# Score tables stored node by node and read in one transfer, edge types checked on ScalarE, a different order at the ends of the second stage

## The chip, the cores and the metric

The kernel runs on one core of a Trainium2 chip. The time is device microseconds from launch to end, the median of the runs shown. One more execution was taken by the hardware profiler; all durations below are from it.

## The reference

Four graph layers on a batch of 128 graphs of 128 nodes with 128 features each; every layer is `x = x + layer(relu(layernorm(x)), adj)`. The first layer is the one that the change is about:

```python
D = abs(x[:, :, None, :] - x[:, None, :, :])        # every pair of nodes
h = einsum('bijc,oc->bijo', D, W1) + b1             # 64 channels
m, v = mean(h, (0, 1, 2)), var(h, (0, 1, 2))        # over the whole batch
h = leaky((h - m) / sqrt(v + EPS) * g1 + be1)       # slope 0.01
s = einsum('bijo,uo->biju', h, W2)[..., 0] + b2
s = where(adj > 0, s, NEG)
y = (softmax(s) @ x) @ Wg.T + bg
y = leaky((y - mean(y, (0, 1))) / sqrt(var(y, (0, 1)) + EPS) * gg + beg)
out = concat([x, y], 2) @ Wt.T + bt
```

Layers 1 and 2 are attention over the same edges with eight heads and with one. Layer 3 picks one of eight score matrices by the value of `adj`, where -1 means no edge. The inputs of this case hold only 0 and 1, so that two of the eight types are enough. The kernel decides that at run time from a number called `types`.

## The kernel before

**Stage A** (0 to about 1255 us) works through pairs of nodes. Scores are symmetric, so each graph needs only half its pairs: node i with the 63 or 64 nodes that follow it, cyclically. A graph's 128 nodes are cut in NQ = 4 quarters of QR = 32; `block(b, q)` makes the absolute differences of one quarter in a tile `d` (VectorE at L541 or GpSimd at L544, then ScalarE at L547), multiplies by W1 in `ph` (TensorE, L558) and copies to `v` (ScalarE, L568); VectorE takes the statistics (L573). A graph's `v` (128 x 4064 floats, 2032 KB) goes to DRAM (L522). The last KEEP = 8 graphs stay in SBUF, in the 8 buffers of the pool `pairs`.

**Stage B** (about 1263 to 2107 us) turns pairs into attention, 8 graphs (GS) to a *score table*, 16 tables, the first one for the graphs that are still in SBUF. For each graph (`graph_scores`): load `v` (SyncE's queue, L654); normalise two parts of 1528 columns on ScalarE (L659), leaky on VectorE (`leaky_part`, L418); a relu of the last quarter on ScalarE (L663); 20 matmul records of TensorE (L684) that add the graph's rows to the table's PSUM bank `sc`. For each table (`score_table`): VectorE adds a bias to make `us` (L703); four DMAs of GpSimd's queue, one for each quarter, write `us` to a DRAM tile `s` in a skewed pattern (L713); four more read it back as rows of nodes, `u` (L726), each to 32 partitions. DRAM is the place where columns of pairs become rows of nodes. Then `attention` for each half table of 4 graphs: GpSimd folds the columns (L767), TensorE sums with the transpose and the mask in `pl` (L774 to L777), softmax on VectorE and ScalarE (L782 to L792), two more matmuls, and `yt` is stored (L808) with its statistics (L812). The generator `edges` brings `adj` (L738) and h (L753) of 4 graphs, makes the mask `negm` on VectorE (L742), and on GpSimd adds a*a - a of each edge number to `sum_odd` in four operations (L746 to L750). After the last table VectorE and TensorE reduce `sum_odd` to `types` (L836 to L841).

**Stage C** (about 2107 us to the end) starts with a branch on `types` (L1306). `layers` then runs the rest in 32 groups of 4 graphs. `load(g)` issues four DMAs (L981 to L987) into pool `c_in` with 3 buffers of each; group g's generator asks for group g+1.

The order of instructions of TensorE, ScalarE, VectorE and GpSimd is fixed ahead by `in_order`. It is a planner: generators yield an engine, a planned duration, and the buffers taken and freed, and the planner always emits the step that can begin first by its own clock. `yield "wait", t` only moves that clock. Each engine then executes its list strictly in that order, so a step planned too early blocks all that stands behind it. In `score_table` the planned waits are 3.0 after the writes and 14.0 after the reads. SyncE is not planned; its DMAs go out in program order. GpSimd's own DMAs stand in GpSimd's list.

Of the kernel before, what the change touches and what calls it, by code (L numbers as in the profile page):

```python
# [9 lines left out]
F32 = mybir.dt.float32  # L10
I32 = mybir.dt.int32
# [148 lines left out]
def kernel(ctx: ExitStack, tc: tile.TileContext, x, adj, w, out):  # L160
# [46 lines left out]
    nc.sync.dma_start(w_slide[0:64, 30:31], w2_col)  # L207
    nc.sync.dma_start(w_slide[64:128, 31:32], w2_col)
# [157 lines left out]
    QS = GS * QR * (W + 1)  # L366
    scores_d = [dram.tile([NQ, QS], F32, tag=f"s{i}", name=f"s{i}") for i in range(2)]

# [47 lines left out]

    def leaky(engine, out, v, slope):
        engine.scalar_tensor_tensor(out, v, slope, v, ALU.mult, ALU.max)  # L418
# [4 lines left out]
    with tc.tile_pool(name="h_pool", bufs=1) as h_pool, tc.tile_pool(name="pairs", bufs=B_V) as b_v:  # L423
# [10 lines left out]
        with tc.tile_pool(name="a2", bufs=2) as a2, tc.tile_pool(  # L434
# [13 lines left out]
            zero = a_d.tile([P, QR * 64], F32, tag="d", name="zero")[:, 0 : NQ * QS // P]  # L448
            nc.gpsimd.memset(zero, 0.0)
            for sd in scores_d:  # L450
                flat_sd = bass.AP(
                    tensor=sd.tensor, offset=sd.offset, ap=[[NQ * QS // P, P], [1, NQ * QS // P]]
                )
                nc.sync.dma_start(flat_sd, zero)
# [71 lines left out]
            def block(b, q, made):  # L526
# [22 lines left out]
                ph = a_ph.tile([P, 2, 512], F32, tag="ph", name="ph")  # L549
                for part in range(1 if q else 4):  # L550
                    for t in range(2):
                        for a in range(2):
                            k = (2 * t + a) * n
                            if part == 0:
                                wt, x_ = w1T if q else w1T2, d[:, k : k + n]
                            else:
                                wt, x_ = us[:, part - 1, :], both[:, k : k + n]
                            nc.tensor.matmul(  # L558
                                ph[64 * a : 64 * a + 64, t, 0:n], wt, x_,
                                start=part == 0, stop=q > 0 or part == 3,  # L560
                            )
# [20 lines left out]
            with tc.manual_schedule(engines=ORDERED):  # L582
# [19 lines left out]
                po, own[0:64, :], w_slide[0:64, 30:31].to_broadcast([64, GS * QR]),  # L602
# [3 lines left out]
            for sd in scores_d:  # L606
                for q in range(NQ):
                    diagonal = bass.AP(
                        tensor=sd.tensor, offset=sd.offset + q * QS + QR * q,
                        ap=[[QS, 1], [W + 1, GS * QR]],  # L610
                    )
                    nc.sync.dma_start(diagonal, own_row)


        with tc.tile_pool(name="b2", bufs=2) as b2p, tc.tile_pool(name="b_s", bufs=2, space=PSUM) as b_s, tc.tile_pool(
            name="b_ps", bufs=6, space=PSUM
        ) as b_ps:
            scores, tables, masks = {}, {}, {}
            sum_odd = b2p.tile([P, GB, P], F32, tag="sum_odd", name="sum_odd", bufs=1)
            nc.gpsimd.memset(sum_odd, 0.0)  # L620
# [10 lines left out]
                shift_ps, h_bi[0:64, :].to_broadcast([64, P]), w_slide[0:64, 30:31],  # L631
# [9 lines left out]
            def leaky_part(part, n):  # L641
                yield DVE, 0.15 + 0.00112 * n, "", ""
                leaky(nc.vector, part, part, 0.01)

            def graph_scores(order, i):
# [3 lines left out]
                if b in here:  # L649
                    v = here.pop(b)  # L650
                else:
                    yield DMA, 5.9, "v", ""
                    v = b_v.tile([P, NPAIR], F32, tag="v", name="v")
                    nc.sync.dma_start(v, pairs_d[b])  # L654
                lin = first[NQ - 1]
                for a, e in ((0, lin // 2), (lin // 2, lin)):
                    yield ACT, 0.2 + 0.00092 * (e - a), "", ""
                    part = v[:, a:e]
                    nc.scalar.activation(part, part, AF.Identity, bias=h_bi, scale=h_sc)  # L659
                    yield "fork", leaky_part(part, e - a)  # L660
                yield ACT, 1.1, "r", ""
                r = b2p.tile([P, 1024], F32, tag="r", name="r", bufs=B_R)
                nc.scalar.activation(  # L663
                    r[:, 0 : NPAIR - lin], v[:, lin:NPAIR], AF.Relu, bias=h_bi, scale=h_sc
                )
                yield "join",
                if i:
                    yield "after", ("w2", order[i - 1])
# [4 lines left out]
                for t in range(2):  # L673
                    k = 2 * (b % GS) + t
                    begins, ends = i == t == 0, i == GS - 1 and t == 1
                    for q in [*range(NQ), NQ]:
                        rows = slice(QR * min(q, NQ - 1), QR * min(q, NQ - 1) + QR)
                        n = 8 * width[min(q, NQ - 1)]
                        if q < NQ:
                            z = v[:, first[q] + t * n : first[q] + t * n + n]  # L680
                        else:
                            z = r[:, t * n : t * n + n]
                        wz = w_slide if q < NQ - 1 else w_line if q < NQ else w_relu
                        nc.tensor.matmul(  # L684
                            sc[rows, 0:n], wz[:, 30 - 2 * k : 62 - 2 * k], z,
                            start=begins and q < NQ, stop=ends and q != NQ - 1,
                            tile_position=(0, rows.start),
                        )
# [4 lines left out]
            def score_table(k):  # L693
# [14 lines left out]
                for q in range(NQ):  # L708
                    skewed = bass.AP(
                        tensor=sd.tensor, offset=sd.offset + q * QS + QR * q + 1,  # L710
                        ap=[[8 * (W + 1), QR], [W + 1, 8], [1, width[q]]],
# [8 lines left out]
                yield POOL, 2.6, "", "us"  # L720
                for q in range(NQ):
                    by_row = bass.AP(
                        tensor=sd.tensor, offset=sd.offset + q * QS,
                        ap=[[W, QR], [QR * (W + 1), GS], [1, W]],
                    )
                    nc.gpsimd.dma_start(u[QR * q : QR * q + QR], by_row)  # L726
                tables[k] = u
                yield "wait", 14.0
# [4 lines left out]
            def edges(g):  # L733
# [9 lines left out]
                yield POOL, 3.8, "", "adj"  # L743

                adf = b2p.tile([P, GB, P], F32, tag="adf", name="adf", bufs=1)
                nc.gpsimd.tensor_copy(adf, adjs)  # L746
                odd = b2p.tile([P, GB, P], F32, tag="odd", name="odd", bufs=1)
                nc.gpsimd.tensor_tensor(odd, adf, adf, ALU.mult)
                nc.gpsimd.tensor_tensor(odd, odd, adf, ALU.subtract)
                nc.gpsimd.tensor_tensor(sum_odd, sum_odd, odd, ALU.add)  # L750
# [11 lines left out]
                yield "done", ("edges", g)  # L762

            def attention(g, u):
# [43 lines left out]
                nc.gpsimd.dma_start(y_d[g], yt)  # L808
                yield DVE, 1.5, "", "yt"
# [3 lines left out]
                nc.vector.bn_aggr(y_mv[:, g, :], y6.rearrange("p a b -> p (a b)"))  # L813

            makers = []

            for k in [NB // GS - 1, *range(NB // GS - 1)]:
                makers += [partial(edges, k * GS // GB + g) for g in range(GS // GB)]
                order = sorted(range(GS * k, GS * k + GS), key=lambda b: b not in here)
                makers += [partial(graph_scores, order, i) for i in range(GS)]  # L820
                makers.append(partial(score_table, k))
            two = dict.fromkeys(("sc", "us", "adj", "negm", "zg", "e", "eT", "yt", "ht"), 2)
            with tc.manual_schedule(engines=ORDERED):
# [3 lines left out]

            n_parts = NB // GB
            mean, var = mean_var(
                b2p, [(1.0 / n_parts, y_mv[:, :, 0], y_mv[:, :, 1])], n_parts  # L830
            )
            affine(b2p, y_sc, y_bi, mean, var, None, gg, beg)


            odd_p = b2p.tile([P, 1], F32, tag="odd_p", name="odd_p")
            nc.vector.tensor_reduce(odd_p, sum_odd.rearrange("p g j -> p (g j)"), AX.X, ALU.max)  # L836
            pt = b_ps.tile([1, P], F32, tag="pb", name="odd_ps")
            nc.tensor.transpose(pt, odd_p, ident)
            odd_1 = b2p.tile([1, 1], F32, tag="odd_1", name="odd_1")
            nc.vector.tensor_reduce(odd_1, pt, AX.X, ALU.max)  # L840
            nc.vector.tensor_scalar(types, odd_1, 1.0, None, ALU.min)  # L841
# [5 lines left out]
    def layers(simple):  # L847

        with tc.tile_pool(name="c_in", bufs=3) as c_in, tc.tile_pool(
# [126 lines left out]
            loaded = {}  # L976

            def load(g):
                b0 = g * GC
                xg = c_in.tile([P, GC, P], F32, tag="xg", name="xg")  # L980
                nc.sync.dma_start(xg, x_t[:, b0 : b0 + GC, :])  # L981
                ad = c_in.tile([P, GC, P], I32, tag="adj", name="adj")
                nc.sync.dma_start(ad, adj_t[:, b0 : b0 + GC, :])
                yt = c_in.tile([P, GC, P], F32, tag="yt", name="yt")
                nc.sync.dma_start(yt, y_d[g])
                ht = c_in.tile([P, GC, P], F32, tag="ht", name="ht")
                nc.sync.dma_start(ht, h_d[g])  # L987
                loaded[g] = xg, ad, yt, ht
# [95 lines left out]
            def group(g):  # L1084
                b0 = g * GC
                xg, ad, yt, ht = loaded.pop(g)
                if g + 1 < NB // GC:
                    load(g + 1)
# [210 lines left out]
            load(0)  # L1299
# [49 lines left out]
```

## Time and profile before

| | us |
|---|---|
| median of 3 runs | 3228.68 (3226.74 to 3233.18) |
| the profiled execution | 3225.39 |
| its span, first to last instruction | 3223.1 |

| window | length | TensorE busy | VectorE busy | ScalarE busy | GpSimd busy |
|---|---|---|---|---|---|
| 0 to 1200 | 1200 | 1093.20 | 1157.88 | 1154.19 | 1092.99 |
| 1290 to 1690 | 400 | 327.62 | 299.94 | 309.51 | 130.06 |
| 1690 to 2050 | 360 | 296.39 | 264.10 | 271.38 | 131.30 |
| 2170 to 3130 | 960 | 906.66 | 771.52 | 759.12 | 209.57 |

A busy time that is close to its window's length marks the engine that sets the pace there. Where none is close, as in the second and third rows, waits set it.

### The profile page before, as it was taken

The numbers are of one execution on the slowest core, as the hardware profiler recorded it, in microseconds if no ns is written. First come the engines' busy times: TensorE is split into PE (matmuls) and PEld (weight loads), VectorE is DVE, ScalarE is ACT, GpSimd is POOL, SyncE is SP. The second block draws the span as 40 slices with busy tenths as digits, with TensorE's granted clock in tenths as the row PEclk, the third lists the DMA queues.
The fourth block names the chain that finished last, engine by engine and source line by source line (L and its number), as shares of the span: only waits on it lengthen the run. The fifth ranks groups of instructions, "written<-read, shape, count | busy, mean of one in ns | idle before, by whom it ended". The sixth has DMA issues, their size and how long they took to land.

```text
span 3223.1 us, 46662 instructions
## 1 busy us (share of the span) xinstructions
PE 2841.3 (88%) x17077; PEld 1552.3 (48%) x17129; DVE 2683.3 (83%) x4729; ACT 2656.7 (82%) x3018; POOL 1666.3 (52%) x1130
## 2 busy tenths in 40 slices
PE   6999999999999997878788887779999999999996
PEld 2333333333333332323333333357777787877875
DVE  6999999999999998868677786567787888887864
ACT  5999999999999998968687777547777777877774
POOL 5999999999999996233324233221222122312211
PEclk8999999999999998989999999879999999999997
DMA  3565555555555541999999999340111111111000
GB/s 126 232 248 227 230 237 233 233 222 246 245 227 231 235 188 60 394 374 388 374 375 396 365 394 371 129 124 11 43 47 38 43 37 43 44 40 40 11 11 12
DMA packets 151743, 606.48 MB, mean 188 GB/s; under 512 B 16401, under 2 KB 99794, under 8 KB 120786
## 3 DMA queue, kind: packets, MB, share of 16 engines
q1 hardware_dynamic: 140242, 569.86, 45.8%
q0 software_dynamic: 11264, 33.53, 3.2%
q8 instruction: 140, 2.29, 0.3%
q14 instruction: 97, 0.79, 0.1%
HBM read 322.74 MB, written 280.61 MB: 187 GB/s over the span
## 4 chain that ended last, share of the span: by engine, by line
PE 21%; DVE 17%; DMA 13%; ACT 4%; issue 4%; POOL 2%; SPq 0%; POOLq 0%; DVEq 0%; ACTq 0%
DMA u<-s 7%; PE pa L1052 6%; DMA s<-us 4%; DVE v L418 3%; PE po L964 2%; DVE p L920 1%; PE ps L1071 1%; PE pp L1064 1%; PE z L916 1%; PE pl L774 1%; PE ph L1194 1%; DVE s L886 1%; DVE e L792 1%; POOL s L713 1%; DVE xh L973 1%
## 5 line engine op out<-in xcount | busy, mean ns | idle before, releaser
L544 POOL TENSOR_TENSOR d<-he 128x2016 f32<-128x2016 f32 (+1 forms) x288 | 1021.8, 3576 | 74.7 <-ACT v L568 62.4
L558 PE MATMUL ph<-d,w1T 128*64 128x512 f32 (+1 forms) x4096 | 934.9, 595 | 85.2 <-ACT d L547 41.0
L547 ACT ACTIVATE d<-d 128x2016 f32<-128x2016 f32 (+1 forms) x384 | 740.6, 1931 | 0.1
L573 DVE BATCH_NORM_STATS2 six<-v 128x6 f32<-128x504 f32 (+1 forms) x1024 | 631.7, 671 | 8.2 <-ACT v L568 5.0
L558 PEld LDWEIGHTS ph<-d,w1T 128*64 128x64 f32 x4096 | 296.5, 137 | 621.0 <-issue 366.4
L568 ACT COPY v<-ph 128x1024 f32<-128x1024 f32 (+1 forms) x512 | 517.4, 1035 | 10.6 <-PE ph L558 10.4
L893 POOL TENSOR_TENSOR rs<-ve,nhalf 128x4 f32<-128x4 f32 x96 | 120.0, 1250 | 777.2 <-DVE ve L890 595.8
L541 DVE TENSOR_TENSOR d<-he,pt 128x2048 f32<-128x2048 f32 (+1 forms) x224 | 506.2, 2260 | 9.7 <-PE ph L558 9.7
L418 DVE SCALAR_TENSOR_TENSOR v<-v 128x1528 f32<-128x1528 f32 x256 | 439.8, 1763 | 28.6 <-ACT v L659 28.1
L659 ACT ACTIVATE v<-v,h_bi,h_sc 128x1528 f32<-128x1528 f32 x256 | 410.7, 1652 | 7.0 <-DVE h_bi L415 7.0
L684 PE MATMUL sc<-v,w_slide 128*32 128x512 f32 (+1 forms) x1536 | 334.7, 604 | 42.5 <-DVE v L418 42.5
L1052 PE MATMUL pa<-vals,p 128*128 128x99 f32 (+2 forms) x2048 | 259.2, 283 | 15.6 <-DVE p L920 11.6
L1052 PEld LDWEIGHTS pa<-vals,p 128*128 128x128 f32 x2048 | 253.5, 200 | 33.8 <-DVE p L920 15.4
L684 PE MATMUL sc<-v,w_line 128*32 128x504 f32 x512 | 262.1, 594 | 0.0
L684 PE MATMUL sc<-r,w_relu 128*32 128x504 f32 x512 | 259.1, 588 | 0.0
L920 DVE SCALAR_TENSOR_TENSOR p<-p,q 128x1024 f32<-128x1024 f32 (+1 forms) x192 | 205.6, 1078 | 49.6 <-ACT q L1039 24.8
L558 PE MATMUL ph<-both,us 128*64 128x512 bf16 x1536 | 189.3, 379 | 0.0
L1038 ACT ACTIVATE p<-z 128x1024 f32<-128x1024 f32 x128 | 133.3, 1041 | 38.2 <-PE z L916 37.8
L782 DVE TENSOR_REDUCE mx<-pl 128x4 f32<-128x512 f32 x32 | 21.9, 685 | 170.4 <-PE pl L777 170.4
L786 ACT ACTIVATE e<-e 128x512 f32<-128x512 f32 x32 | 20.2, 631 | 172.8 <-DVE e L784 172.8
L558 PEld LDWEIGHTS <-us 128*64 128x64 bf16 x1536 | 100.6, 110 | 116.8 <-issue 73.2
L663 ACT ACTIVATE r<-v,h_bi,h_sc 128x1008 f32<-128x1008 f32 x128 | 156.2, 1221 | 0.8 <-PE sc L684 0.8
(255 smaller groups left out, 4693.4 us busy)
## 6 DMA issues: line engine op xcount, KB each, us to landing
v<-v SPq DMA_DIRECT2D x240, 2032.0 KB, 9.1
xg<-in_x SPq DMA_DIRECT2D x64, 256.0 KB, 3.1
ht<-h SPq DMA_DIRECT2D x64, 256.0 KB, 6.1
u<-s POOLq DMA_DIRECT2D x64, 192.0 KB, 13.2
h<-he SPq DMA_DIRECT2D x32, 256.0 KB, 3.1
adj<-in_adj POOLq DMA_DIRECT2D x32, 256.0 KB, 8.8
y<-yt POOLq DMA_DIRECT2D x32, 256.0 KB, 8.0
adj<-in_adj SPq DMA_DIRECT2D x32, 256.0 KB, 2.9
```

Source lines behind the costliest of these rows:

```text
L418: engine.scalar_tensor_tensor(out, v, slope, v, ALU.mult, ALU.max)
L541: nc.vector.tensor_tensor(dv, later, own, ALU.subtract if q else ALU.max)
L544: nc.gpsimd.tensor_tensor(dv, later, own, ALU.subtract)
L547: nc.scalar.activation(d[:, 0 : 4 * n], d[:, 0 : 4 * n], AF.Abs)
L558: nc.tensor.matmul(ph[64 * a : 64 * a + 64, t, 0:n], wt, x_, start=part == 0, stop=q > 0 or part == 3,)
L568: nc.scalar.copy(v.rearrange("p (t e) -> p t e", t=2), ph[:, :, 0:n])
L573: nc.vector.bn_stats(made["six"][:, 2 * q + t, :], v[:, t * n : t * n + n])
L659: nc.scalar.activation(part, part, AF.Identity, bias=h_bi, scale=h_sc)
L663: nc.scalar.activation(r[:, 0 : NPAIR - lin], v[:, lin:NPAIR], AF.Relu, bias=h_bi, scale=h_sc)
L684: nc.tensor.matmul(sc[rows, 0:n], wz[:, 30 - 2 * k : 62 - 2 * k], z, start=begins and q < NQ, stop=ends and q != NQ - 1, tile_position=(0, ...
L920: nc.vector.scalar_tensor_tensor(p, p, FLOOR, q, ALU.max, ALU.max)
L1052: nc.tensor.matmul(pa_all[:, h * (DH + 1) : h * (DH + 1) + n], p[:, h, :], vals_all[:, e : e + n], start=True, stop=True,)
```

## The change

- The DRAM tile of a table is now 128 rows of 8 x 193 floats, a row for each node, and the 8 graphs lie one after the other in it. The read is one DMA with 128 partitions in place of four with 32; both read 1024 pieces of 768 bytes. The writes stay four DMAs of the same 256-byte pieces, but a partition's 8 pieces now lie in rows that are 4 nodes apart, and neighbouring partitions are 772 bytes apart.
- For that, stage A's matmuls take rows r, r+4, r+8, ... of a quarter (a strided view of `d` and `both`) instead of 8 rows in sequence, and W2 is put in other columns of `w_slide`.
- The planned costs change: after the read 8.0 instead of 14.0, its issue 1.2 instead of 2.6, the `v` load 5.2 instead of 5.9, a leaky part 0.00105 instead of 0.00112 for each column. The relu and the normalising steps become forks of their own.
- `edges` forks `of_types`: one ScalarE operation, the sum over a row of (a - 0.5) squared, in place of the four on GpSimd. A row with only 0 and 1 gives 128, anything else more.
- `y_norm`, `edge_types` and `first_inputs` become chains in the planner. The last one loads group 0's four inputs of stage C to a pool `late` while stage B still runs; `load(1)` then takes the place of `load(0)`.
- In the first table two graphs are put ahead of the `edges` steps.

```diff
-    QS = GS * QR * (W + 1)
-    scores_d = [dram.tile([NQ, QS], F32, tag=f"s{i}", name=f"s{i}") for i in range(2)]
+    ROW = GS * (W + 1)
+    scores_d = [dram.tile([P, ROW], F32, tag=f"s{i}", name=f"s{i}") for i in range(2)]
...
+                every4 = "p (r x j) -> p x r j"
+                by_part = d[:, 0 : 4 * n].rearrange(every4, x=4, j=w_)
+                both_by_part = both.rearrange(every4, x=4, j=64)
...
-                            k = (2 * t + a) * n
+                            k = 2 * t + a
                             if part == 0:
-                                wt, x_ = w1T if q else w1T2, d[:, k : k + n]
+                                wt, x_ = w1T if q else w1T2, by_part[:, k]
                             else:
-                                wt, x_ = us[:, part - 1, :], both[:, k : k + n]
+                                wt, x_ = us[:, part - 1, :], both_by_part[:, k]
...
                     skewed = bass.AP(
-                        tensor=sd.tensor, offset=sd.offset + q * QS + QR * q + 1,
-                        ap=[[8 * (W + 1), QR], [W + 1, 8], [1, width[q]]],
+                        tensor=sd.tensor, offset=sd.offset + QR * q * ROW + 1,
+                        ap=[[W + 1, QR], [4 * ROW, 8], [1, width[q]]],
                     )
...
                 yield "wait", 3.0
-                yield POOL, 2.6, "", "us"
-                for q in range(NQ):
-                    by_row = bass.AP(
-                        tensor=sd.tensor, offset=sd.offset + q * QS,
-                        ap=[[W, QR], [QR * (W + 1), GS], [1, W]],
-                    )
-                    nc.gpsimd.dma_start(u[QR * q : QR * q + QR], by_row)
-                tables[k] = u
-                yield "wait", 14.0
+                yield POOL, 1.2, "", "us"
+                by_row = bass.AP(
+                    tensor=sd.tensor, offset=sd.offset, ap=[[ROW - 1, P], [W + 1, GS], [1, W]]
+                )
+                nc.gpsimd.dma_start(u, by_row)
+                yield "wait", 8.0
...
-                yield POOL, 3.8, "", "adj"
...
-                nc.gpsimd.tensor_copy(adf, adjs)
-                odd = b2p.tile([P, GB, P], F32, tag="odd", name="odd", bufs=1)
-                nc.gpsimd.tensor_tensor(odd, adf, adf, ALU.mult)
-                nc.gpsimd.tensor_tensor(odd, odd, adf, ALU.subtract)
-                nc.gpsimd.tensor_tensor(sum_odd, sum_odd, odd, ALU.add)
+                yield "fork", of_types(g, adjs)
...
+            def of_types(g, adjs):
+                yield ACT, 0.65, "", "adj"
+                nc.scalar.activation(
+                    adjs.bitcast(F32), adjs, AF.Square, bias=nhalf[:, 0:1], accum_out=squares[:, g : g + 1]
+                )
+                to_see.remove(g)
+                if not to_see:
+                    yield "done", "types"
...
+            def first_inputs():
+
+                yield "after", ("loaded", order[-1])
+                for dst, src in zip(early, inputs(0)):
+                    if src is y_d[0]:
+                        yield "after", ("stored", 0)
+                    yield DMA, 0.6, "", ""
+                    nc.sync.dma_start(dst, src)
...
+                n = 0 if makers else 2
+                makers += of_graphs[:n] + of_edges + of_graphs[n:] + [partial(score_table, k)]
+            makers += [y_norm, edge_types, first_inputs]
...
-            load(0)
+            load(1)
```

## The prediction

> **What bounds the kernel now.** First the windows by stage, for where an engine is full. Stage A has VectorE at 1157.88 and ScalarE at 1154.19 of 1200 us, stage C TensorE at 906.66 of 960: the change takes nothing from either. Stage B between 1300 and 2050 us has no full engine, so I went to the waits of 1180 to 2200 us (columns: engine and line, whom it waited for, us in total, times, longest).
>
> ```profile
> engine line waited for: us in total, times, longest us
> POOL u L767 <- DMA u<-s: 223.4, 16, 22.2
> ...
> ACT e L786 <- DVE e L784: 172.8, 17, 17.1
> DVE mx L782 <- PE pl L777: 170.4, 16, 17.7
> PEld pl L774 <- POOL u L767: 117.6, 15, 13.4
> ...
> DVE odd_p L836 <- POOL sum_odd L750: 12.2, 1, 12.2
> ```
>
> Once for each table all engines stop in a chain: GpSimd for the read of `u`, TensorE for GpSimd, VectorE for TensorE, ScalarE for VectorE. Each stop is about 10 us of 51.3 (tables begin their writes at 1308.01 and 14 tables later at 2026.53). The lists are fixed, so this is attention that stands in them before its data has come. No engine waits for a load of `v`. The chain of waits shows what they wait for, twice over:
>
> ```profile
> 1721.82 8.18 DMA s<-us
> 1730.55 17.42 DMA u<-s
> 1748.90 2.07 PE pl L774 x2
> 1770.15 11.09 DMA s<-us
> 1781.53 13.73 DMA u<-s
> 1796.20 2.07 PE pl L774 x2
> ```
>
> Over the 14 tables the last leg of the read averages 15.7 us. Then the windows, narrow (columns: TensorE, weight loads, VectorE, ScalarE, GpSimd busy, clock, DMA share, GB/s):
>
> ```profile
> 1720.00:1730.00 10.00, 9.38 (x56) 2.69 (x55) 9.49 (x6) 10.00 (x8) 4.08 (x7) 1.00 1.02 420
> ...
> 1730.00:1745.00 15.00, 10.44 (x58) 2.73 (x50) 10.23 (x6) 14.39 (x11) 0.59 (x1) 1.00 1.01 300
> ```
>
> The DMA share is full in both, but while `u` is read the core moves 300 GB/s and not 420: the read slows the loads beside it. So DMA is a second limit just behind the waits. A table moves 8 x 2032 KB of `v`, 1536 KB of adj, h and y, 768 of `u` and 254 of `us`, 19.3 MB: at 420 GB/s 45.9 us, plus 4.3 lost in the read (15 x 120/420), about 50. That is the measured period within 1.1.
>
> **The change part by part, per table.**
>
> *The read.* Four issues (0.59 each, spaced by the four writes' arrivals, 3.9 us from first to last) become one. The 4.5 MB moved in those 15 us would take 10.7 at 420: 4.3 less. The nearest row for a 128-partition transfer on GpSimd's queue is adj: its issue takes 0.79, and the window 1710 to 1720, with an adj load (issued at 1708.20) under way, moved 420 GB/s. Against the gain: no quarter can be read before the last write has landed, and one issue of 1024 pieces lasts longer (0.8 by adj's row, 1.2 by the planner's number). [...] The trace's loss of 4.3 is of loads as well[...]; I take 4.3, less 0.3 for the two counter-effects: **-4.0**, between +1 (nothing but the new wait and the pieces) and -7.
>
> *The writes.* Same four issues, bytes and pieces, other addresses. 7.0 and 8.7 us to landing now; no row shows scattered ones. I take 0, -1 to +2.
>
> *The place of attention.* The planner's path from writes to attention shrinks by 1.4 + 6.0 = 7.4 us, so attention moves ahead. Now TensorE does alternately 6 and 5 graphs (20 records each of L684) between a table's end and the next `pl`. From `pl` to the next table's end:
>
> ```profile
> 1748.90 2.07 PE L774 MATMUL pl<-u,ident 128*128 128x512 f32 x2 [7.42 <-POOL u L767]
> 1767.50 1.45 DVE L703 TENSOR_SCALAR us<-sc,b_rows 64x512 f32<-64x512 f32 x2
> ...
> 1796.20 2.07 PE L774 MATMUL pl<-u,ident 128*128 128x512 f32 x2 [7.08 <-POOL u L767]
> 1821.03 1.45 DVE L703 TENSOR_SCALAR us<-sc,b_rows 64x512 f32<-64x512 f32 x2
> ```
>
> 18.6 us with 6 done before, 24.8 with 5: a graph that moves behind the stop costs 6.2. A planned load of 5.2 makes graphs denser in the plan, which gives part of the 7.4 back: I take half a graph (5 and 5), **+3.1**; bounds 0 and 1.5 graphs, 0 to +9.3.
>
> *Edge types.* Four GpSimd operations (0.80 + 1.04 + 1.43 + 1.27, twice a table) go. GpSimd has room, so their own time is worth nothing. But they stand just after `pl`, beside VectorE's hardest stretch, where it runs without a gap from `pl` on. There VectorE's two operations on 512 columns are stretched:
>
> ```profile
> L792 DVE TENSOR_TENSOR e<-e,ri 128x512 f32<-128x512 f32 x28 | 27.8, 994 | 1.0
> L742 DVE TENSOR_SCALAR negm<-adj 128x512 f32<-128x512 int32 x28 | 27.1, 966 | 0.0
> ```
>
> Their minima are 691 and 416 ns. Two of each per table: 2 x (0.30 + 0.55) = **-1.7**, 0 at the least. ScalarE gets two squares, by the row of the nearest copy (`zg`, 0.59) 1.2 us a table. Its cover is the gaps that it has behind VectorE in this stretch (1.96 us at 1758); without them +1.2. The square frees the adj buffer; GpSimd's next adj load waits already for VectorE's mask.
>
> *Stage A.* TensorE reads rows of 64 floats that are 4 rows apart. Nearest row: `pl` L774 reads 128-float runs with a gap, 592 ns at the least, against 595 for L558's unbroken 512. So 0. If shorter runs cost 10%, TensorE would go from 1093 to about 1200 of 1200 us and some 20 us would show. The zero fill and the diagonal's DMAs are as many as before.
>
> Sum for a table: -4.0 + 3.1 - 1.7 = -2.6, and 14 tables **-36**. The period of 48.7 stays above DMA's 45.9.
>
> **The ends.** *Last table:* VectorE stood 12.2 us at L836 for GpSimd's checks, with the last graphs' leaky parts queued behind it; the chain of waits runs through all eight GpSimd operations (2044.69 to 2053.41, 8.7 us). The new check stands in the planner. I take -8 (-12 to -4). *First table:* the masks (1269.00 and 1270.39) stood between VectorE's first leaky parts and waited for adj, which took 4.36 us; TensorE's first long run of L684 came at 1274.09, the first `v` load followed it, and at 1299.24 ScalarE waited for a `v` with the table's end behind it. Two graphs ahead: -4 (-8 to +1). *Stage C:* the branch came at 2106.40, then
>
> ```profile
> 2108.35 5.51 DMA yt<-y
> ...
> 2113.97 0.82 ACT yl L1096
> ```
>
> With group 0's inputs there, `yl` waits only for `y_bi` (2110.27 + 0.22), 3.4 us sooner, and three buffers then hold groups 1 to 3, not 0 to 2, which helps the `yt` and `xg` waits that follow (2119.51, 2125.60). The four early DMAs are 1 MB behind the last `v` load, 2.5 us of a queue that is empty by then. -6 (-12 to 0). Together **-18**.
>
> -36 - 18 = -54 on the execution's 3225.39: 3171. The median of the runs stands 3.3 above that execution, so 3175.
>
> **The rivals.** *Attention too early (slower).* The plan moves by 7.4 whatever the read really does. If it moves by a whole graph (+6.2) and the read gains only 1 us, a table costs 6.2 - 1 - 1.7 = +3.5; 14 tables +49, less 18: about +31, 3260. For: the engines wait already, and the stop is in their lists. Against: the rate of 300 in the read. It decides from the point where a moved graph costs more than the read gains plus 1.7 plus 1.3 (the ends over 14 tables): 3.2 us of gain for a whole graph.
>
> *DMA is the bound, and the stop goes.* If the read is so short that attention is ready at its place, the period falls to DMA's floor plus slack, say 46.5: 14 x -4.8 = -67, less 18, -85: 3144. For: share of 1.0 all through stage B; VectorE and ScalarE are busy 38 to 39 of 51.3 (264.10 and 271.38 of the 360 us from 1690). Against: 4 us off a 30 us path from `us` to `pl` leave a stop.
>
> *Nothing in stage B.* The read's loss is of its pieces, not of its 32 partitions; the shorter wait and the later slots cancel. Only the ends: -18, 3211.
>
> **How the numbers follow.** A difference below 0.2% (6.5 us) can't be told from none here. Forecast 0.36, DMA bound 0.26, ends only 0.19, too early 0.16, strided reads in stage A 0.03. Faster: 0.36 + 0.26 + 0.15 of the ends' 0.19 + 0.02 of the too-early case = 0.79; slower: 0.13 of the too-early case + 0.01 of the strided one = 0.14; same: what is left of the three, 0.07. The range takes the DMA case with its ends at their best (about 3120) and the first part of the slower rival: to 3238.
>
> **What would show it.** Right: GB/s stays near 400 while `u` is read; `u` issues 16, not 64; tables begin their writes about 49 us apart; L792 and L742 near 0.70 and 0.42; no wait at the end of edge types; `yl` in stage C waits for no `yt` at first. Wrong: the stop at L786 still 10 us or more with 4 graphs ahead of `pl`; a rate of 300 as before; L558 above 600 ns; stage A beyond 1260 us.

## The result, and the profile after

Over the runs of both kernels on one chip the median falls from 3230.9 to **3180.2 us**; the ratio is 0.985, 95% interval [0.981, 0.989]. That is faster by 1.5%, well over the 0.2% that can be told from no change. The profiled execution has a span of 3171.4 us (3223.1 before).

Added lines shift the numbers: the read of `u` is now L738, GpSimd's addition L780, `pl` L787 to L790, the maximum L795, `exp` L799, the table's end (`us`) L717, `negm` L753, the product with the reciprocals L805, the square L770.

The waits of 1180 to 2150 us (engine and line, whom it waited for, us in total, times, longest):

```profile
engine line waited for: us in total, times, longest us
...
POOL u L780 <- DMA u<-s: 163.1, 16, 11.2
ACT e L799 <- DVE e L797: 149.3, 29, 26.8
DVE mx L795 <- PE pl L790: 142.5, 29, 20.4
POOL adj L749 <- ACT adj L770: 141.6, 16, 11.0
...
PEld pl L787 <- POOL u L780: 116.7, 16, 16.9
```

The chain of stops is the one of before, in the same order, and shorter: GpSimd stands 163 us for the read and not 223. It has not gone. The new wait for the square (L770) shows no cost: it delays loads of adj that are early anyway, and `negm` doesn't wait for them in this stretch. The timeline of TensorE and VectorE shows what is left of a stop (in brackets the idle time just before):

```profile
1650.54 1.52 DVE L717 TENSOR_SCALAR us<-sc,b_rows 64x512 f32<-64x512 f32 x2 [0.95 <-PE sc L698]
1675.22 2.08 PE L787 MATMUL pl<-u,ident 128*128 128x512 f32 x2 [5.93 <-POOL u L780]
1699.09 1.52 DVE L717 TENSOR_SCALAR us<-sc,b_rows 64x512 f32<-64x512 f32 x2 [0.95 <-PE sc L698]
1724.61 2.07 PE L787 MATMUL pl<-u,ident 128*128 128x512 f32 x2 [6.78 <-POOL u L780]
1747.69 1.52 DVE L717 TENSOR_SCALAR us<-sc,b_rows 64x512 f32<-64x512 f32 x2 [0.95 <-PE sc L698]
```

From `us` to `pl` it is now 24.7 and 25.5 us (25.2 on the average of 14 tables, 29.6 before), and a table takes 48.6 us. Counted in the records of L698, TensorE does 4.5 graphs in that time, where it did alternately 6 and 5, and still stands some 6 us. A window inside the read that is issued at 1711.76 and lands at 1723.8, and one that begins 2 us before it lands (TensorE, weight loads, VectorE, ScalarE, GpSimd busy, clock, DMA share, GB/s):

```profile
1714.00:1722.00 8.00, 3.83 (x20) 1.12 (x18) 5.27 (x4) 7.79 (x6) 0.00 (x0) 0.93 1.01 401
1722.00:1730.00 8.00, 5.39 (x18) 3.40 (x19) 0.98 (x2) 0.00 (x0) 1.40 (x2) 0.65 1.03 427
```

The drop to 300 GB/s is gone: the first window lies inside the read and moves 401. VectorE's two stretched operations, in the groups by form, are close to their minima of before (691 and 416 ns):

```profile
L805 DVE TENSOR_TENSOR e<-e,ri 128x512 f32<-128x512 f32 x32 | 22.1, 692 | 1.1
L753 DVE TENSOR_SCALAR negm<-adj 128x512 f32<-128x512 int32 x32 | 13.6, 424 | 1.0 <-DMA adj<-in_adj 1.0
```

Where the 51.7 us of span went, by the starts of `us` and of `yl`: the first table's end comes at 1308.6 (1.6 us later than before), 14 periods save 38.8 us, the last table 11.8, and from there to the end 2.8.

### The profile page after: what moved, and what is told of

The parts are those of the page before. It is cut to its first block, busy times and chain, and to the rows that moved or that the text cites. A ratio compares the mean times of both kernels' runs of the same rounds, so it can differ in the third digit from the quotient of the medians.

```text
span 3171.4 us, 46611 instructions
## 1 busy us (share of the span) xinstructions
PE 2832.2 (89%) x17129; PEld 1559.5 (49%) x17129; DVE 2657.7 (84%) x4730; ACT 2673.4 (84%) x3082; POOL 1495.2 (47%) x953
## 4 chain that ended last, share of the span: by engine, by line
PE 27%; DVE 13%; issue 7%; ACT 5%; POOL 2%; DMA 1%; POOLq 0%; DVEq 0%; ACTq 0%
PE pa L1091 5%; PE sc L698 4%; PE po L1006 2%; DVE p L962 2%; PE z L958 1%; PE ps L1110 1%; PE pl L787 1%; PE pp L1103 1%; PE ph L1233 1%; DMA s<-us 1%; PE pl L789 1%; DVE s L928 1%; DVE v L425 1%; DVE xh L1015 1%; DVE f1d L1194 1%
## 5 line engine op out<-in xcount | busy, mean ns | idle before, releaser
L565 PE MATMUL ph<-d,w1T 128*64 128x512 f32 (+1 forms) x4096 | 939.8, 596 | 83.1 <-ACT d L551 40.6
L565 PEld LDWEIGHTS ph<-d,w1T 128*64 128x64 f32 x4096 | 306.4, 136 | 613.7 <-issue 385.3
L425 DVE SCALAR_TENSOR_TENSOR v<-v 128x1528 f32<-128x1528 f32 x256 | 433.9, 1742 | 32.8 <-ACT v L653 32.2
L698 PE MATMUL sc<-v,w_slide 128*32 128x512 f32 (+1 forms) x1536 | 321.4, 599 | 17.2 <-DVE v L425 16.9
L1091 PEld LDWEIGHTS pa<-vals,p 128*128 128x128 f32 x2048 | 249.2, 197 | 32.7 <-DVE p L962 15.1
L698 PE MATMUL sc<-v,w_line 128*32 128x504 f32 x512 | 260.3, 590 | 0.0
L698 PE MATMUL sc<-r,w_relu 128*32 128x504 f32 x512 | 258.2, 586 | 0.0
L565 PE MATMUL ph<-both,us 128*64 128x512 bf16 x1536 | 190.5, 381 | 0.0
L565 PEld LDWEIGHTS <-us 128*64 128x64 bf16 x1536 | 100.9, 111 | 117.7 <-issue 74.6
L799 ACT ACTIVATE e<-e 128x512 f32<-128x512 f32 x32 | 20.2, 630 | 149.3 <-DVE e L797 149.3
L698 PEld LDWEIGHTS sc<-v,w_slide 128*32 128x32 f32 x1536 | 65.1, 109 | 158.9 <-DVE v L425 82.5
```

Source lines behind the costliest of these rows:

```text
L565: nc.tensor.matmul(ph[64 * a : 64 * a + 64, t, 0:n], wt, x_, start=part == 0, stop=q > 0 or part == 3,)
L698: nc.tensor.matmul(sc[rows, 0:n], wz[:, 31 - k : 63 - k], z, start=begins and q < NQ, stop=ends and q != NQ - 1, tile_position=(0, rows.st ...
L1091: nc.tensor.matmul(pa_all[:, h * (DH + 1) : h * (DH + 1) + n], p[:, h, :], vals_all[:, e : e + n], start=True, stop=True,)
```

## The experiments

Twelve kernels were run, each made from the changed one by the edit shown. The table gives the median, the ratio to the kernel before in the same session (interval in the text where it decides), and from the profile the distance from the start of the first table's `us` to that of the last one's (15 tables; the changed kernel's 720.3 is 48.0 a table), and the GB/s from 1315 to 1960 us.

| kernel | us | ratio | first to last `us` | GB/s |
|---|---|---|---|---|
| before | 3230.9 | 1 | 770.8 | 380 |
| changed | 3180.2 | 0.985 | 720.3 | 400 |
| e1: read in 4 x 32 partitions | 3217.2 | 0.996 | 761.0 | 376 |
| e5: read in 2 x 64 partitions | 3223.0 | 0.998 | 764.5 | 373 |
| e2: read in 4 x 2 graphs, 128 partitions | 3163.5 | 0.978 | 705.2 | 408 |
| e14: read in 2 x 4 graphs, 128 partitions | 3154.6 | 0.977 | 703.2 | 409 |
| e3: attention later | 3153.9 | 0.976 | 698.0 | 411 |
| e4: edge types on GpSimd | 3293.0 | 1.018 | 832.1 | 352 |
| e12: e4, stores of `y` by ScalarE | 3223.0 | 0.998 | 761.3 | 379 |
| e13: e4 with e3 | 3194.0 | 0.989 | 732.2 | 395 |
| e6: late verdict on the types | 3179.6 | 0.984 | 723.5 | 397 |
| e8: no early inputs | 3186.7 | 0.985 | 729.7 | 394 |
| e9: e2 with e3 | 3150.7 | 0.975 | 692.3 | 412 |
| e10: e9 with e6 | 3146.2 | 0.974 | 690.9 | 411 |

### The read: e1, e5, e2, e14

```diff
...
-                nc.gpsimd.dma_start(u, by_row)
+                for q in range(NQ):      # e1: 4 x 32; e5: 2 x 64 in the same way
+                    by_row = bass.AP(
+                        tensor=sd.tensor, offset=sd.offset + QR * q * (ROW - 1),
+                        ap=[[ROW - 1, QR], [W + 1, GS], [1, W]],
+                    )
+                    nc.gpsimd.dma_start(u[QR * q : QR * q + QR], by_row)
```
```diff
...
-                nc.gpsimd.dma_start(u, by_row)
+                for q in range(4):       # e2; e14: range(2) with 4 graphs each
+                    by_row = bass.AP(
+                        tensor=sd.tensor, offset=sd.offset + 2 * q * (W + 1),
+                        ap=[[ROW - 1, P], [W + 1, 2], [1, W]],
+                    )
+                    nc.gpsimd.dma_start(u[:, 2 * q : 2 * q + 2, :], by_row)
```

Expected of e1: 

> The changed kernel, but each table is read in four transfers of 32 partitions again, out of the new layout. Theory 'partitions' (the gain of the read is that one transfer spans all 128 partitions[...]): the read's last piece lands some 4 us later than the 12.0 us of the changed kernel, the way from the start of us to pl grows from about 25 to 29 us, the period of a table from 48.6 to about 52 us, the time from 3180 to 3230 to 3250 us. Rival 'layout' (what counts is that a row of the table lies together in memory, however many transfers fetch it): all four land at about 12 us, period 48.6 +/- 0.5 us, time 3175 to 3190 us.

Expected of e5: 

> The changed kernel with the table read in two transfers of 64 partitions and all eight graphs. Theory 'partitions' [...]: between the changed kernel and e1, 3190 to 3210 us, with a GB/s between 376 and 400 in the window of e1. Rival [...]: like the changed kernel, 3173 to 3188 us.

Expected of e2: 

> The changed kernel, but each table is read in four transfers of all 128 partitions, two graphs each: as many transfers as in e1, none on fewer partitions. Theory 'partitions': near the changed kernel, with at most 3 x 0.9 us for three more issues on GpSimd per table (half of which can be hidden, since the first four graphs need only the first two transfers): period 48.5 to 50 us, time 3175 to 3205 us, and clearly below e1. Rival 'number of transfers' [...]: like e1, 3230 to 3250 us.

Expected of e14: 

> The changed kernel with the table read in two transfers of all 128 partitions and four graphs each, one for each group of attention. Theory 'first half' (e2's gain of 17 us comes from the first group's half that lands earlier): like e2, us to pl 23 us, period 47.4 us, 3158 to 3170 us. Rival 'transfers in flight' (four transfers at once take a larger share of the DMA engines against the loads of v): half of the gain or less, 3170 to 3180 us.

The partitions of a transfer decide, not the layout and not the number of transfers. e1 (four transfers) and e5 (two) lose 37 and 43 us against the changed kernel; e2 (four) and e14 (two), on all partitions, win 17 and 26. The sizes were off: e1 was expected at 3230 or more and came to 3217.2; e5 was expected between the changed kernel and e1 and is no better than e1; e2 was expected at 3175 or more and came to 3163.5, and e14 at 3158 or more and came to 3154.6. The windows from 1315 to 1960 us, first of the changed kernel, then e1, e5 and e14, show in their last two columns how:

```profile
1315.00:1960.00 645.00, 546.24 (x2982) 222.99 (x2976) 490.98 (x529) 530.82 (x481) 95.35 (x144) 0.93 1.00 400
```
```profile
1315.00:1960.00 645.00, 517.12 (x2785) 212.40 (x2783) 459.01 (x492) 496.85 (x448) 109.29 (x176) 0.90 1.01 376
```
```profile
1315.00:1960.00 645.00, 513.37 (x2768) 210.77 (x2769) 456.07 (x489) 494.20 (x446) 95.93 (x148) 0.90 1.01 373
```
```profile
1315.00:1960.00 645.00, 566.53 (x3035) 232.43 (x3028) 497.81 (x538) 537.87 (x488) 107.12 (x161) 0.93 1.01 409
```

The DMA share is full in all four (1.00 or 1.01). What differs is the bytes moved in it, so a full share doesn't tell the rate. One read each of the changed kernel, e1 and e5 shows where the bytes are lost:

```profile
1712.00:1723.00 11.00, 5.83 (x30) 1.59 (x24) 7.27 (x5) 9.79 (x8) 0.65 (x1) 0.90 1.01 399
```
```profile
1731.00:1750.00 19.00, 10.12 (x58) 3.12 (x50) 11.56 (x7) 14.08 (x11) 2.34 (x4) 0.83 1.02 314
```
```profile
1733.00:1751.00 18.00, 8.85 (x47) 2.64 (x43) 10.29 (x7) 12.82 (x10) 1.37 (x2) 0.82 1.02 282
```

Over 13 tables of each trace, counted from a table's first read issue to its last landing, the core moves 402 GB/s in the changed kernel, 304 in e1 and 295 in e5; in the rest of the time it is 399, 417 and 415. e1's read is itself only 44 of the 304, and the changed kernel's 68 of the 402. So it is the loads beside a narrow read that pay most, and only while it lasts. (The medians of `v` from issue to landing, 15.1 us in the changed kernel and 22.6 in e1, do not measure this loss: they are 31.4 us in e9, which moves the most.) Why 64 partitions are no better than 32 was not shown.

e2 and e14 show one thing more. A read in two by graphs lets the first group's addition and `pl` wait for one half only: from `us` to `pl` 23.4 us on the average, TensorE's wait at `pl` 62.3 us over 14 tables in e14 against 86.4 in the changed kernel, the period 47.3. e2's four transfers win the same in this stage (705.2 against 703.2), so the halves are what matters and not more transfers in flight. The 9 us between their medians are not separated: their intervals, [0.9765, 0.9793] and [0.9755, 0.9786], overlap.

### The place of attention: e3

```diff
-                yield POOL, 1.2, "", "us"
+                yield POOL, 2.6, "", "us"
...
-                yield "wait", 8.0
+                yield "wait", 14.0
```

> The changed kernel with the planner told of the read as it was before (2.6 us of GpSimd and a wait of 14.0 us in place of 1.2 and 8.0), so that attention comes one to two graphs later in TensorE's order. Theory 'place' (the 6 us that TensorE still stands at pl per table come from attention being ordered too early): graphs ahead of pl go from 4.5 to about 6, the stop at pl from 6.1 to 1 us or less per table, the period from 48.6 to 45.9 to 47 us (it can't go under what the DMA engines need, about 45.9), the time to 3145 to 3165 us. Rival 'DMA is the bound' (the stop only moves to the next wait, for v): period and time as in the changed kernel, 3172 to 3190 us. Rival 'too late' (scores or u tiles are held longer and the scores of the next table wait): slower, 3195 us or more.

The time is the one expected of "place", 3153.9 us, ratio 0.976 [0.975, 0.978], and the period is 46.7; the rest of that theory fell. The graphs ahead of `pl` alternate between 5 and 7, and the stop didn't vanish. The waits of e3 from 1310 to 1990 us:

```profile
...
DVE mx L795 <- PE pl L790: 107.5, 16, 9.5
POOL u L738 <- DMA s<-us: 105.6, 9, 13.5
...
PE pl L787 <- POOL u L780: 70.5, 14, 6.8
```

TensorE still stands 5.0 us a table, because the path from `us` to `pl` has grown from 25.2 to 30.5 us: GpSimd waits longer for the writes to land (medians of 9.4 and 11.2 us, 7.4 and 8.3 in the changed kernel). Why they land later is open. The stage moves 411 GB/s, near the most of all runs. But from the third table to the last but one a load of adj or a store of `y` also leaves 0.5 to 0.7 us ahead of the writes on GpSimd's queue (in one table 3.8 us), where in the changed kernel it is mostly 8; in the changed kernel's only table with such a neighbour, at 1358.3, the writes took 9.5 to 11.4 us too. The place is worth 1.5 us a table (22.3 us over 15) for one and a half graphs, not the whole stop.

### Edge types: e4, e12, e13

```diff
...
-                yield "fork", of_types(g, adjs)
+                yield POOL, 3.8, "", "adj"
+                adf = adjs.bitcast(F32)
+                nc.gpsimd.tensor_copy(adf, adjs)
+                nc.gpsimd.tensor_tensor(adf, adf, adf, ALU.mult)
+                nc.gpsimd.tensor_tensor(adf, adf, adf, ALU.mult)
+                nc.gpsimd.tensor_tensor(early[2], early[2], adf, ALU.add)
...
```

In e4 alone the running sum is still added to after the early `y` input has been put in the same tile, so the first group's inputs are changed; e12 and e13 load that input after the verdict. All three differ in one more way from the kernel before: they work in the tile of adj itself, so the first of the four operations has to wait until VectorE has made its mask from it. e12 has besides:

```diff
-                yield POOL, 0.7, "", ""
-                nc.gpsimd.dma_start(y_d[g], yt)
+                yield ACT, 0.7, "", ""
+                nc.scalar.dma_start(y_d[g], yt)
```

Expected of e4: 

> The changed kernel with the edge types on GpSimd again, four operations of 128x512 per group of four graphs (a copy to floats, two products and a sum, in place; the sum is of fourth powers, which stands for the old check), and no Square on ScalarE. Theory 'VectorE is stretched by GpSimd and it counts': negm goes from 425 back to about 960 ns and the product with the reciprocals from 692 to about 990 ns, 1.7 us per table, and each lies on the way to the next wait: +24 us, time 3200 to 3208 us. Rival 'hidden': the same stretch of the two VectorE operations, but VectorE waits at mx 8.7 us per table anyway, so the time stays within 6 us of 3180 us. Rival 'ScalarE gains': without the 0.9 us of Square per group ScalarE ends its exp earlier and the time falls by up to 20 us.

Expected of e12: 

> e4 (edge types on GpSimd, four operations per group), but the stores of y are issued by ScalarE, right behind the operation that makes them, in place of GpSimd; the early y input is loaded after the verdict on the types. In e4 the stores of y stood behind GpSimd's operations and went out 2 to 6 us ahead of the writes of the table's scores, on the same queue; these writes then landed in 14.1 us (median of the last eight tables) in place of 8.2. Theory 'queue': with the stores out of the way the writes land in 8 to 10 us, the way from us to pl falls from 33.7 to 25 to 27 us, the period from 60 to 49 to 51 us: 3190 to 3215 us. Rival 'GpSimd's work itself' (it stretches VectorE and delays the next loads of adj wherever the stores are): 3260 us or more.

Expected of e13: 

> e4 with the planner's old numbers of e3, so that attention, and with it the stores of y, come later; the early y input is loaded after the verdict on the types. Theory 'the parts depend on each other' (edge types on GpSimd cost 113 us only together with the early attention): e3's 3154 us and the 1.7 us of stretched VectorE operations for 14 tables, 3170 to 3190 us. Rival 'edge types on GpSimd cost this much wherever attention stands': 3240 us or more.

e4 missed by far: 113 us slower than the changed kernel, where 24 or nothing was expected, and slower than the kernel before, which also has four such operations on GpSimd. GpSimd's timeline in e4 shows the wait for the mask, and then what stands just ahead of the writes:

```profile
1728.80 0.61 POOL L755 CAST adj<-adj 128x512 f32<-128x512 int32 x1 [6.66 <-DVE negm L752]
...
1742.63 2.83 POOL L758 TENSOR_TENSOR yt<-yt,adj 128x512 f32<-128x512 f32 x1
1745.41 0.60 POOL L828 DMA_DIRECT2D y<-yt  x1
1746.64 0.75 POOL L748 DMA_DIRECT2D adj<-in_adj  x1 [0.64 <-issue]
1747.38 0.56 POOL L828 DMA_DIRECT2D y<-yt  x1
1749.14 2.33 POOL L726 DMA_DIRECT2D s<-us  x4 [1.20 <-DVE us L716]
1766.55 0.89 POOL L737 DMA_DIRECT2D u<-s  x1 [15.09 <-PE sc L697]
```

The same stretch of the changed kernel:

```profile
1641.74 0.56 POOL L821 DMA_DIRECT2D y<-yt  x1 [3.43 <-ACT yt L819]
1642.43 0.75 POOL L749 DMA_DIRECT2D adj<-in_adj  x1
1643.50 0.56 POOL L821 DMA_DIRECT2D y<-yt  x1 [0.32 <-ACT yt L819]
1651.58 2.33 POOL L727 DMA_DIRECT2D s<-us  x4 [7.52 <-DVE us L717]
1662.54 0.89 POOL L738 DMA_DIRECT2D u<-s  x1 [8.63 <-PE sc L698]
```

In the kernel before, the first operation follows the fold at once:

```profile
1691.67 1.40 POOL L767 TENSOR_TENSOR u<-u 128x256 f32<-128x256 f32 x2 [13.20 <-DMA u<-s]
1693.01 0.60 POOL L746 CAST adf<-adj 128x512 f32<-128x512 int32 x1
```

From 1315 to 1960 us the wait for the mask comes to 77.2 us in e4, 75.1 in e12 and 82.4 in e13, where before only the next load of adj waits for the mask, 24.6 us in the same window. How much of the times of these three kernels is due to it was not separated, so they are no clean price of the edge types.

With attention early, `y` is ready while GpSimd works on the types. Its two stores of 256 KB and a load of adj then leave 2 to 4 us ahead of the scores' writes on the same queue, where the changed kernel leaves 8 to 10. The writes land late and the read is issued 17.4 us after them, not 11. (The labels at the read name TensorE; the chain of waits has these 15.09 us as DMA s<-us.) Medians from issue to landing over the whole run, for e4, the changed kernel and e12:

```profile
s<-us POOLq DMA_DIRECT2D x32, 64.0 KB, 12.1
```
```profile
s<-us POOLq DMA_DIRECT2D x32, 64.0 KB, 7.4
```
```profile
s<-us POOLq DMA_DIRECT2D x32, 64.0 KB, 6.5
```

(The medians of 14.1 and 8.2 in e12's expectation mixed writes and reads of the table; of the writes alone, e4's 64 KB pieces land in 13.9 us from 1700 to 2050.) e12 takes the stores off this queue, and 70 of the 113 us come back: the writes land in 6.5 us and `us` to `pl` is mostly 24 to 27 us. That stores close ahead delay the writes is shown by it. That the shared queue does it is not: in e12 the stores also leave earlier, mostly 5 to 7 us ahead of the writes. And e4 itself has a table whose stores stand on GpSimd's queue, 4 and 5 us ahead:

```profile
1572.97 0.56 POOL L828 DMA_DIRECT2D y<-yt  x1
1574.35 0.56 POOL L828 DMA_DIRECT2D y<-yt  x1 [0.82 <-ACT yt L826]
1578.23 2.34 POOL L726 DMA_DIRECT2D s<-us  x4 [3.33 <-DVE us L716]
1589.46 0.90 POOL L737 DMA_DIRECT2D u<-s  x1 [8.88 <-PE sc L697]
```

There the writes landed in 6.3 to 8.8 us; in the eight tables behind it, with stores 2 to 4 us ahead, they took 12.6 to 16.1. What remains, 43 us, fits neither range of e12 (3190 to 3215, and 3260 or more). VectorE may be part of it: `v` (L425, 16 times a table) rises from 1738 to 1854 ns, `negm` from 425 to 818 and the product with the reciprocals from 692 to 1287 (1315 to 1960 us), together 16 x 0.12 + 2 x 0.39 + 2 x 0.60 = 3.9 us a table. That is more than the 2.7 us a table lost, so not all of it is on the path; the wait for the mask is the other candidate. e13 ties e4's loss to attention's place: with the later slots the types cost 40 us (3194.0 against e3's 3153.9), not 113, though more than the 16 to 36 expected.

### The ends: e6, e8

In the changed kernel SyncE passes the branch early and issues twelve loads for groups 1 to 3 from 2031.93 to 2041.56, while the last table is read. The chain of waits and then the windows there:

```profile
2031.66 3.77 DMA s<-us
2036.00 8.91 DMA u<-s
```
```profile
2036.00:2040.00 4.00, 0.00 (x0) 0.00 (x0) 0.00 (x0) 0.00 (x0) 0.89 (x1) 0.50 0.99 299
2040.00:2045.00 5.00, 0.00 (x0) 0.00 (x0) 0.00 (x0) 0.00 (x0) 0.02 (x1) 0.50 1.07 333
```

No engine computes for 9 us, and the DMA engines are full with loads that nothing needs so soon. e6 holds them back:

```diff
             def edge_types():
-                yield "after", "types"
+                yield "after", ("pl", 29)
...
+                yield "done", ("pl", g)      # in attention, behind pl
                 yield DVE, 1.4, "e", "pb"
```

> The changed kernel, but the verdict on the edge types, for which every engine waits at the branch ahead of the last stage, is taken only after the last table's pl. SyncE then passes the branch some 14 us later and can't issue the last stage's twelve loads (3 MB) while the last table is read. Theory 'collision' (these loads slow the last read): the last read lands about 5.5 us after its issue instead of 8.9, and the last us to the first yl takes 35 to 37 us instead of 39.0: about -3 us, 3173 to 3180 us. Rival 'the read takes what it takes': still 8.9 us, the same time. Rival 'late branch' (the reduction, the transpose and the flag now stand between the last pl and the branch, and the loads of the second group come late): slower by 2 to 6 us.

The chain of waits of e6:

```profile
2035.98 2.92 DMA s<-us
2039.47 5.30 DMA u<-s
```

The collision is real: 5.3 us and not 8.9, and from the last `us` to `yl` 33.2 us and not 39.0. But the median is the same (3179.6; 0.984 [0.983, 0.986]): from `yl` to the end it took 1111.3 us, where the changed kernel took 1103.5. The late loads do show in e6: the third and fourth group's `yl` wait for their `y` and start 3.5 and 6.6 us after the first one, against 1.4 and 2.1 in the changed kernel. That this delays the end is not shown, as the next run tells. e10 against e9 is the same pair once more: 5.2 us sooner at `yl`, 5.0 us longer after it, with overlapping intervals ([0.9729, 0.9755], [0.9733, 0.9771]).

e8 is without the early inputs:

```diff
-            makers += [y_norm, edge_types, first_inputs]
+            makers += [y_norm, edge_types]
...
-            loaded = {0: early}
+            loaded = {}
...
-            load(1)
+            load(0)
```

> The changed kernel without the early inputs: the first group's four inputs are loaded behind the branch, ahead of those of the others, as before the change; the rest as changed. If the early inputs are worth what the first stretch of the last stage shows (5.6 us less from the first yl to the end, and an earlier yl), the way from the last us to the first yl grows by 2 to 6 us and the time is 3183 to 3190 us. Rival 'hidden' (SyncE is past the branch 40 us before yl, so the loads land in time all the same): 3176 to 3183 us, with the same distances.

Nothing is settled: 3186.7 us, but the ratio 0.985 [0.983, 0.987] lies on the changed kernel's. From the last `us` to `yl` it is 38.6 us (39.0), so the early inputs did not bring `yl` forward; to the end it is then 1109.2 against 1103.5. Over the twelve kernels, nearly all with an unchanged last stage, this last distance ranges from 1102.4 (e9) to 1112.7 (e2), so one profile can't tell 6 us there.

### Together: e9, e10

These are the edits of e2 and e3, and in e10 that of e6 as well.

Expected of e9: 

> The changed kernel with both of what e2 and e3 did: four transfers of all partitions for a read, and the planner's old numbers, which put attention one to two graphs later. Theory 'the DMA engines are now the bound' (19.3 MB per table at the 412 GB/s of e3 are 46.7 us, which is e3's period): period 46.3 to 46.8 us, time 3145 to 3156 us, and the stop at pl is replaced by waits for v. Theory 'the gains add' (-17 of the read and -26 of the place): period about 45.6 us, time 3135 to 3142 us. Theory 'they exclude each other': later than e3, 3158 us or more.

Expected of e10: 

> e9 with the late verdict of e6 as well. If the collision at the last table is real, 2 to 4 us less than e9 with a last read of 5 to 6 us; if it isn't, the same as e9; if the late branch costs, 2 to 6 us more than e9.

The gains don't add: e9 has 3150.7 us, as "the DMA engines are the bound" had it. Its first two tables come fast (38.7 and 42.5 us), the thirteen behind them average 47.0, and 19.3 MB at 412 GB/s are 46.8. The stage moves hardly more than e3 with 411, and the theory's sign is there too, a wait of ScalarE for loads of `v` (1310 to 1990 us), which the changed kernel and e3 do not have; TensorE's stop at `pl` goes on, smaller:

```profile
1315.00:1960.00 645.00, 570.71 (x3126) 225.16 (x3126) 518.34 (x556) 561.13 (x505) 136.94 (x195) 0.97 1.01 412
```
```profile
ACT v L653 <- DMA v<-v: 64.0, 49, 2.8
...
PE pl L789 <- POOL u L782: 55.7, 20, 7.0
```

Both versions beat the changed kernel, e10 with 3146.2 us by 34.

## Why the prediction was right or wrong

**What bounds the kernel: right.** The stop for `u` was the chain, and DMA stood just behind it. The changed kernel kept the shape of the stop, and e3 and e9 then ran into DMA at 411 and 412 GB/s. The floor of 45.9 us, worked out at 420, was a little too low: at 412 the same 19.3 MB are 46.8, about the period of e3 (46.7).

**The read, -4.0 a table: right in kind, too large by a third.** `us` to `pl` fell by 4.4 us, but e1 and e5, which undo the read alone, give back 2.7 and 2.9 us a table (40.7 and 44.2 over 15). The runs show that the partitions of a transfer decide: from 1315 to 1960 us the core moves 400 GB/s with 128, 373 with 64 and 376 with 32; why, they don't show. Most of the loss is of the loads beside the read, as I had taken it from the trace: while the read lasts, 74 of the 98 GB/s that e1 moves less than the changed kernel. The 0.3 us for counter-effects was my estimate and was not separated: no run reads the old rows in one transfer.

**The writes, 0: right** (7.4 and 8.3 us to landing, 7.0 and 8.7 before), though e4 shows that this rests on what leaves just ahead of them, which I had not looked at.

**The place of attention, +3.1: right in sign, wrong in both factors.** I had half a graph move (5.5 ahead on the average, then 5), and a whole one did (4.5). And e3, which puts one and a half graphs ahead again, makes them 1.5 us a table, so a graph is worth about 1 us and not 6.2. I had priced it as if the path from `us` to `pl` stayed as long; in e3 it grew by 5.3 us.

**Edge types, -1.7: the stretch was right to a hundredth (0.692 and 0.424 us), its worth is not settled.** With e3's order e13 costs 2.3 us a table (34.2 over 15); with the early attention of the change e12 costs 2.7 and e4 7.5. All three are more than 1.7, but all three carry the wait for the mask, which the kernel before does not have. What e4 and e12 do show is that this price depends on the order of the rest: the stores of `y` close ahead of the writes were no part of my sum. Attention early with the types left on GpSimd came out slower than the kernel before (e4); that was a rival of its own which I did not see.

**The sum came out by luck: two terms erred against each other.** The read gained 1.3 us a table less than forecast and the place of attention cost about 1.6 less. The single steps by e1, e3 and e13 are -2.7 + 1.5 - 2.3 = -3.5 us a table; measured from first to last `us` it is (720.3 - 770.8) / 15 = -3.4, of which the last table has a larger share. The two agree so well by chance as well, since e3 moves more than the change did and e13 has the wait for the mask. For 14 periods it is -38.8 us against the -36 forecast.

**The ends, -18: measured -13.** The last table gave -11.8 for -8: the 12.2 us at the end of the checks went whole. The first table gave +1.6 for -4: `h_bi`, made at the end of stage A, came 3.4 us later, and the rest is -1.8; two graphs first was not tried alone. The last stage gave -2.8 for -6. It was taken as free of cost that SyncE issues its loads early, and they slowed the last read from about 5.3 to 8.9 us; but e6, without this, ends no sooner, so where the other 3 us went is open. **Stage A, 0: right within what one profile can tell.** L565 takes 598 and 595 ns, L558 took 597 and 592. But in all 13 profiles of kernels with the change `h_bi` comes 2.8 to 6.1 us later than in the one of before, so a few microseconds may be lost there.

**The rivals.** "Attention too early" did not come true, but not because the read gained enough: a whole graph moved, and the read's 2.7 to 2.9 us are less than the 3.2 that I had set for that. A moved graph was simply cheaper. Attention placed early made the kernel slower than before only in e4, with the types on GpSimd, and there mostly through the late writes (70 of the 113 us) and not through the price of a moved graph. "DMA is the bound" is not the changed kernel but the versions that go on from it. "Nothing in stage B" and "strided reads" are out by the periods and by L565.

## What to carry to other kernels

Span all 128 partitions with a transfer that runs beside a stream of loads (here the stage moved 400 GB/s with such a read, 376 and 373 with reads on 32 and 64), and cut it, if at all, along the free axis where its consumers are cut (409 with two halves). When work is ordered earlier, look at which transfers it then puts just ahead of others that are waited for: here moving the stores of `y` away from the scores' writes was worth 70 us, more than the whole change. Single terms of a sum hold only in the order in which they were measured.

## What was unexpected of the hardware

A read on 64 partitions (373 GB/s over the stage) was no better than one on 32 (376), against 400 for all 128, with a DMA share of 1.00 to 1.01 in each: a full share went with 295 GB/s during such a read and with 402 during the wide one, so it doesn't tell what is moved. And two stores of 256 KB with a load, put 2 to 4 us and not 8 us ahead of four small writes on GpSimd's queue, went with a landing in 13.9 us and not 7.4.
